# Graph layer on one core: x + h of one row block stored from another buffer, the first load of x in two halves, the last product in two pieces of columns

## The chip, the cores and the metric

The kernel runs on one core of one Trainium2 chip. The metric is the device time of one execution in microseconds (us). Three executions of the kernel before took 1384.38, 1384.48 and 1384.94 us; the median is 1384.48 us. Engines are named as in the profile: PE is TensorE (matmul), PEld its weight load, DVE is VectorE, ACT is ScalarE, POOL is GpSimd, and SP is SyncE, which here only issues DMAs.

## The reference

One layer of a relational graph network with a highway gate, in float32, on N = 1250 nodes with D = 1024 features, E = 20000 edges and R = 8 edge types:

```python
h = relu(layernorm(x))                      # over the 1024 features, no scale or shift
u = h @ root + bias
for r in range(8):                          # mean over the edges of type r into a node
    sums = segment_sum(h[src] * (type == r), dst)
    u += (sums / max(count_r, 1)) @ weight[r]
z = concat([u, h]) @ w_gate + b_gate        # w_gate has 2048 rows
out = x + tanh(u) * z + h * (1 - z)
```

Most of the work is eleven matrix products of 1250 x 1024 by 1024 x 1024: one for each edge type, one with root, and two with the halves of w_gate.

## The kernel before

**Blocks and pairs.** The 1250 rows are ten blocks of 128 (the last has 98). Blocks i and i + 5 are pair i, and are called part 0 and part 1 of the pair. The edge sums are taken after the product: h @ weight[r] is formed for every node and stored in `y`, and a later stage gathers the rows that the edges name and adds them up.

**One product.** `product` multiplies a pair (256 rows) by a 1024 x 1024 matrix with the seven products of a Strassen-like scheme on a 2 x 2 split. The left operand of a pair, `h_op[i]`, is one tile with seven slots of [128, 4 x 128]: the transposed quarters A11, A12, A22 and the sums S1, S2, S3 (which first holds A21) and S4. The function `add` issues the four float32 matmuls of one of the seven; in the profile each matmul has two records, so one add is eight records at L204. The order is A11, S1, S2, S4, S3, A12, A22. Adds gather in banks of PSUM, from which ScalarE and VectorE copy or add the quarters of the result into two row tiles; the last, A22, is taken by the function given as `last`. After each of the seven adds `done` calls `between(j)`, in which the work of other engines is written. There are 55 products, eleven matrices for five pairs, one after another on TensorE. The right operand's sums are made once for each matrix (`make_t1` to `make_t4`, L160 to L172).

**Order.** The order of instructions on each engine is written by hand: it is that of the program text, and the only scheduling is the place at which a piece of work is called. Each engine takes its instructions in order and waits for the semaphores of those it depends on. All loads of x and all stores of rows go over SP's queue.

**The first stage.** The layernorm of all pairs runs beside the first products, from the generator `norms`, which `on` advances by one `yield` after each add. `Normed` holds one block: `xt` its x, `ht` its h. `stats` and `spread` (L388, L392, L393) take mean and deviation, `scale` (L397, L398) the factors, `relu` (L405, on ScalarE) writes h into `ht`, `store` (L410) stores it to `h_dram`, and `with_x` (L414, L415) adds h to x in place and stores the sum to `xh_dram` for the last stage. `both` does this for the two blocks of a pair; `factored` transposes them on TensorE (L180, copied out at L182), and `left` (L189 to L193) makes the sums S1, S2, S4 and S3 on VectorE.

There is little room in SBUF, so blocks use slots of `h_op` tiles that are not yet filled. For pair 2 this matters: x of its first block is loaded into slots S1 and S2 of `h_op[2]` itself, and h of that block is written to `scratch(4, 0)`, slots 0 and 1 of `h_op[4]`. Pair 3's first block later writes its h to the same `scratch(4, 0)`. The second blocks of pairs 2 and 3 share `scratch(4, 1)` in the same way. x of pair 2's second block and of both blocks of pair 3 is in buffers of a pool of three, `xpool`, from which pair 4 takes the buffers for its x and h too.

The order in `norms` around pair 2 is: the x + h of pair 1, then `factored(2)`, the two `with_x` of pair 2, `left(h_op[2])`, the load of x of block 4, and, two yields later, the layernorm of pair 3. The first pair is written by itself ahead of the products, with its relu in two halves; its two blocks are the first loads on SP's queue.

**The last stage.** The eleventh matrix is multiplied with u, which has been gathered by then. `finish` takes half a block's columns of the result, multiplies by one factor and adds another (L1144 and L1145), and `scatter_outs` sends rows to the output with an indirect DMA of POOL (L308). In the last product of all, part 1's first half of the columns comes from the A22 add, straight from PSUM through `last`.

Of the kernel before, what the change touches and what calls it, by code (L numbers as in the profile page):

```python
# [19 lines left out]
def tile_rgcn_highway(  # L20
# [30 lines left out]
    nc = tc.nc  # L51
# [3 lines left out]
    P = 128  # L55
    N, D = x.shape
# [3 lines left out]
    KQ = KC // 2  # L60
    Q = D // 2
    ND = -(-N // P)
    NP = ND // 2
# [16 lines left out]
    A11, A12, A22, S1, S2, S3, S4 = range(7)  # L80
# [4 lines left out]
    def nrows(d):  # L85
        return min(P, N - d * P)
# [18 lines left out]
    xh_dram = dram.tile([N, D], F32, name="xh_dram")  # L105
# [9 lines left out]
    def bank():  # L115
        return psum.tile([P, 512], F32, name="ps", bufs=6)
# [57 lines left out]
    def transposed(aop, part, of, n):  # L174

        for half, to in enumerate(((A11, A12), (A21, A22))[part]):
            p = bank().rearrange("p (k f) -> p k f", k=KQ)
            for i in range(KQ):
                k = KQ * half + i
                nc.tensor.transpose(p[:, i, :n], of[:n, k * P:(k + 1) * P], ident[:n, :n])  # L180
            copy = nc.vector.tensor_copy if half else nc.scalar.copy
            copy(aop[:, to, :, :n], p[:, :, :n])  # L182
            if n < P:
                nc.gpsimd.memset(aop[:, to, :, n:], 0.0)

    def left(aop, part=0):

        if part != 3:
            nc.vector.tensor_add(aop[:, S1], aop[:, A21], aop[:, A22])  # L189
            nc.vector.tensor_sub(aop[:, S2], aop[:, S1], aop[:, A11])  # L190
        if part != 1:
            nc.vector.tensor_sub(aop[:, S4], aop[:, A12], aop[:, S2])
            nc.vector.tensor_sub(aop[:, S3], aop[:, A11], aop[:, A21])  # L193

    def product(aop, w, to, between=lambda j: None, last=nc.scalar.copy):


        c11, c12 = to[0][:, :Q], to[0][:, Q:]
        c21, c22 = to[1][:, :Q], to[1][:, Q:]
        step = [0]  # L200

        def add(b, i, fresh=False):
            for k in range(KQ):
                nc.tensor.matmul(b, aop[:, i, k, :], w.of[i][:, k, :], start=(fresh and k == 0),  # L204
                                 stop=(k == KQ - 1), skip_group_check=True)

        def done():
            between(step[0])
            step[0] += 1

        b, c = bank(), bank()
        add(b, A11, True)
        nc.scalar.copy(c11, b)  # L213
        done()
        add(c, S1, True)
        nc.scalar.copy(c22, c)  # L216
        done()
        add(b, S2)
        nc.scalar.copy(c12, b)  # L219
        done()  # L220
        add(c, S4)
        nc.vector.tensor_add(c12, c12, c)  # L222
        done()
        add(b, S3)
        d = rows.tile([P, Q], F32, name="part", bufs=2)
        nc.scalar.copy(d, b)  # L226
        nc.vector.tensor_add(c22, c22, d)  # L227
        done()
        a = bank()
        add(a, A12, True)  # L230
        nc.vector.tensor_add(c11, c11, a)  # L231
        done()
        add(b, A22)
        last(c21, b)  # L234
        done()

    mats = [weight[r] for r in range(R)] + [root, w_gate[D:, :], w_gate[:D, :]]
# [119 lines left out]
    with ExitStack() as early:  # L357
# [3 lines left out]
        first_part = early.enter_context(ExitStack())  # L361
        xpool = first_part.enter_context(tc.tile_pool(name="xpool", bufs=3))

        def load_x(i, part, t=None):
            d = i + part * NP
            n = nrows(d)
            if t is None:
                t = xpool.tile([P, D], F32, name="xt")
            nc.sync.dma_start(t[:n], x[d * P:d * P + n, :])
            return t  # L370

        def scratch(i, part):

            return h_op[i][:, 2 * part:2 * part + 2].rearrange("p a k f -> p (a k f)")

        class Normed:
# [32 lines left out]
                at = slice(self.d * P, self.d * P + self.n)  # L409
                nc.sync.dma_start(h_dram[at, :], self.ht[:self.n])  # L410

            def with_x(self):
                n = self.n
                nc.vector.tensor_add(self.xt[:n], self.xt[:n], self.ht[:n])  # L414
                nc.sync.dma_start(xh_dram[self.d * P:self.d * P + n, :], self.xt[:n])  # L415

        def both(a, b, parts=1):

            a.stats(0)
            a.stats(1)  # L420
            a.spread()
            b.stats(0)
            a.scale()
            a.relu(parts)
            b.stats(1)
            b.spread()
            b.scale()
            b.relu(parts)

        def factored(i, blocks):  # L430
            for part in range(2):
                transposed(h_op[i], part, blocks[part].ht, blocks[part].n)
# [1 line left out]

        warm = xpool.tile([P, 1], F32, name="warm")
        nc.scalar.activation(warm, eps, AF.Sqrt)
        x0 = [load_x(0, part) for part in range(2)]
        fac[0].load_first()
        fac[0].load_b22()
        x1 = [load_x(1, 0, scratch(NP - 2, 0))]  # L440
# [11 lines left out]
        for name, of, pad in (("dst", dst, G * KEYS), ("typ", etype, R), ("src", src, 0)):  # L452
            t = ix0.tile([P, 2, P], I32, name=f"e_{name}")
# [281 lines left out]
        def norms():  # L735
            yield
            yield
            both(*b1)
            fac[0].make_t4()
            for b in b1:  # L740
                b.store()
            yield
            yield
            factored(1, b1)
            left(h_op[1])
            yield
            for b in b0:
                b.with_x()
            x3 = [load_x(3, part) for part in range(2)]
            b2 = [Normed(2 + part * NP, x2[part], scratch(NP - 1, part)) for part in range(2)]  # L750
            both(*b2)
            yield
            for b in b2:
                b.store()
            yield
            for b in b1:
                b.with_x()
            yield
            factored(2, b2)
            for b in b2:  # L760
                b.with_x()
            left(h_op[2])
            x4 = [load_x(4, 0)]
            yield
            yield
            b3 = [Normed(3 + part * NP, x3[part], scratch(NP - 1, part)) for part in range(2)]
            both(*b3)
            yield
            for b in b3:
                b.store()  # L770
            yield
            factored(3, b3)
            left(h_op[3])
            yield
            for b in b3:
                b.with_x()
            x4.append(load_x(4, 1))
            yield
            for part in range(2):
                b = Normed(4 + part * NP, x4[part], xpool.tile([P, D], F32, name="xt"))  # L780
                b.stats(0)
                b.stats(1)
                b.spread()
                b.scale()
                b.relu()
                b.store()
                yield
                transposed(h_op[4], part, b.ht, b.n)
                b.with_x()
                yield  # L790
            left(h_op[4])
            first_part.close()
# [19 lines left out]
    with ExitStack() as edges_part:  # L812
# [12 lines left out]
        fresh = [GOT]  # L825
# [113 lines left out]
        s, i = next(steps)  # L939
        while s <= R0[1]:  # L940
            step(s, i)
            s, i = next(steps)
# [8 lines left out]
        def with_others(e):  # L951
# [6 lines left out]
            for _ in others:  # L958
# [3 lines left out]
        s, i = beside(with_others(edges(0, range(ND), u_back(0))), sum(K[0]) + 1, s, i,  # L962
                      R0[2] - 1)
# [6 lines left out]
        for g in range(1, G - 1):  # L970
            e = edges(g, range(ND), u_back(g))
            s, i = beside(with_passes(e) if g == G - 2 else e, sum(K[g]) + 1, s, i, R0[g + 2] - 1)
# [4 lines left out]
        with tc.If(passes > 0):  # L977
# [30 lines left out]
            with tc.For_i(0, passes, 1):  # L1008
# [9 lines left out]
                for c in range(NCH):  # L1018
                    n = nedges(c)
# [104 lines left out]
        between = spread(in_turn(late, held()), sum(K[LG]) + 2, 7 * ((NM - 2 - s) * NP + NP - i))  # L1124
        while s < NM - 1:
# [8 lines left out]
            s, i = next(steps, (NM, 0))  # L1134

        for i in range(NP):
            t = [rows.tile([P, D], F32, name="row") for _ in range(2)]

            def finish(part, half, of):
                d = 2 * i + part  # L1140
                n = nrows(d)
                at = slice(half * Q, half * Q + Q)
                to = t[part][:n, at]
                nc.vector.tensor_mul(to, of[:n], place_of("d", i, part)[:n, at])  # L1144
                nc.vector.tensor_add(to, to, place_of("z", i, part)[:n, at])  # L1145

            def beside_u(j):
                if i == 0 and j == 0:
                    fac[NM - 1].make_t4()
                gate_rows(i, j)  # L1150
                if j == 1:
                    scatter_outs()
                if i + 2 < NP:
                    gate_load(i + 2, j)
                if j == (3 if i else 5):
                    finish(0, 1, t[0][:, Q:])
                if j == (4 if i else 5):
                    finish(1, 1, t[1][:, Q:])
                if j == 5:
                    finish(0, 0, t[0][:, :Q])  # L1160
                    outs.append((2 * i, t[0]))
                    if i == NP - 1:
                        scatter_outs()
                if i + 1 < NP:
                    gate_u(i + 1, j)

            product(h_op[i % 2], fac[NM - 1], t, between=beside_u,
                    last=lambda to, b: finish(1, 0, b))
            outs.append((2 * i + 1, t[1]))
        scatter_outs()  # L1170
# [22 lines left out]
```

## Time and profile before

| | us |
|---|---|
| median of three executions | 1384.48 |
| the profiled execution | 1385.41 |
| its span in the profile | 1383.6 |
| PE busy | 1364.6 (99%) |
| DVE busy | 861.1 (62%) |
| POOL busy | 630.1 (46%) |
| ACT busy | 339.4 (25%) |
| mean granted TensorE clock | 0.996 of full |

The profile is of one execution of the program, and its times count from the start of the span. Busy times are sums over the instructions of an engine. A line of the waits names the engine and the instruction that waited, what released it, the time in total, how often, and the longest. A line of the timeline has the start, the busy time, the engine, the line of the kernel, the operation, what it writes and reads, and in brackets the idle time before it and what ended that. The granted clock is the share of full speed that TensorE's clock was given. The matmuls L204 are 3080 records with 1343.5 us.

### The profile page before, as it was taken

How to read it: one execution, taken by the hardware profiler on the slowest of the kernel's cores; microseconds unless marked ns; L12 is line 12 of the kernel's file. 1: busy time of each engine (PE TensorE's matmuls, PEld its weight loads, DVE VectorE, ACT ScalarE, POOL GpSimd, SP SyncE). 2: the span in 40 equal slices, each digit the busy share in tenths (PEclk: the TensorE clock that was granted, in tenths of full speed). 3: DMA queues.
4: the chain of work that ended last, by engine and by line, in shares of the span. 5: the costliest groups of instructions: out<-in, count | busy, mean ns of one | idle time of the engine just before them, and what ended most of it. 6: DMA issues, size and time to landing. Idle time of an engine off the chain costs nothing. (4 is left out here: it accounts for less than half of the span.)

```text
span 1383.6 us, 11973 instructions
## 1 busy us (share of the span) xinstructions
PE 1364.6 (99%) x3562; PEld 615.9 (45%) x3562; DVE 861.1 (62%) x1658; ACT 339.4 (25%) x721; POOL 630.1 (46%) x567
## 2 busy tenths in 40 slices
PE   7899999999999999999999999999999999999998
PEld 4444444444444444444444444444444444444443
DVE  7855877887767826456355575654346564557975
ACT  3335656566521111111111111111111111121220
POOL 0002755665560644556575454544417433425641
PEclk9999999999999999999999999999999999999999
DMA  9654764775545256269878756787659845656861
GB/s 328 257 180 114 165 132 129 162 163 138 98 111 179 62 155 201 63 221 220 241 244 288 261 176 217 281 300 273 218 175 334 293 153 180 206 177 237 293 201 57
DMA packets 109863, 272.73 MB, mean 197 GB/s; under 512 B 25890, under 2 KB 27920, under 8 KB 109664
## 3 DMA queue, kind: packets, MB, share of 16 engines
q0 software_dynamic: 48864, 128.60, 28.8%
q1 hardware_dynamic: 39808, 101.38, 24.7%
q10 hardware_dynamic: 21120, 41.95, 9.8%
q8 instruction: 28, 0.46, 0.1%
q14 instruction: 43, 0.35, 0.1%
HBM read 214.20 MB, written 80.65 MB: 213 GB/s over the span
## 5 line engine op out<-in xcount | busy, mean ns | idle before, releaser
L204 PE MATMUL ps<-w,h_op 128*128 128x512 f32 x3080 | 1343.5, 595 | 0.5 <-DVE w L172 0.4
L204 PEld LDWEIGHTS ps<-w,h_op 128*128 128x128 f32 x3080 | 578.7, 190 | 695.4 <-issue 690.8
L845 DVE SCALAR_TENSOR_TENSOR u<-got,w_of,u 128x1024 f32<-128x1024 f32 (+1 forms) x192 | 246.0, 1283 | 200.3 <-DMA got<-y,idx 197.9
L837 POOL DMA_INDIRECT got<-y,idx x202 | 249.3, 1234 | 230.7 <-DVE u L845 140.7
L664 POOL DMA_INDIRECT table<-row_col,at_i x157 | 177.1, 1128 | 159.8 <-DVE at_i L660 68.7
L222 DVE TENSOR_TENSOR row<-row,ps 128x512 f32<-128x512 f32 x55 | 37.7, 685 | 106.3 <-PE ps L204 71.5
L226 ACT COPY part<-ps 128x512 f32<-128x512 f32 x55 | 32.2, 585 | 269.5 <-PE ps L204 269.5
L234 ACT COPY row<-ps 128x512 f32<-128x512 f32 x50 | 29.3, 585 | 255.3 <-PE ps L204 249.6
L213 ACT COPY row<-ps 128x512 f32<-128x512 f32 x55 | 32.1, 584 | 166.7 <-PE ps L204 158.7
L227 DVE TENSOR_TENSOR row<-row,part 128x512 f32<-128x512 f32 x55 | 37.9, 689 | 46.8 <-ACT part L226 46.7
L219 ACT COPY row<-ps 128x512 f32<-128x512 f32 x55 | 32.1, 584 | 137.7 <-PE ps L204 137.7
L216 ACT COPY row<-ps 128x512 f32<-128x512 f32 x55 | 32.1, 584 | 133.3 <-PE ps L204 129.2
L308 POOL DMA_INDIRECT u_dram<-u,node x20 | 29.2, 1462 | 65.5 <-DVE u L845 63.3
L650 DVE SCALAR_TENSOR_TENSOR junk<-k_bc,key_col,before 128x128 f32<-128x128 int32 x157 | 54.9, 350 | 4.2
L339 POOL DMA_INDIRECT node_dram<-ids,pos_i x30 | 37.7, 1256 | 43.5 <-issue 43.5
L718 DVE SCALAR_TENSOR_TENSOR junk<-v_bc,val,one 128x1280 bf16<-128x1280 f32 x30 | 46.5, 1550 | 8.8 <-DMA v_bc<-val_dram 8.1
L590 DVE TENSOR_TENSOR seen<-seen,ps_n 128x110 f32<-128x110 f32 x157 | 42.1, 268 | 15.5 <-PE ps_n L585 11.5
L567 ACT ACTIVATE is_lo<-io,less_lo 128x128 bf16<-128x128 f32 x157 | 50.1, 390 | 0.7 <-DVE row L227 0.7
L231 DVE TENSOR_TENSOR row<-row,ps 128x512 f32<-128x512 f32 x55 | 37.5, 682 | 19.1 <-PE ps L204 19.1
L302 POOL DMA_INDIRECT u<-u_dram,node x20 | 21.7, 1087 | 48.4 <-DMA u_dram<-u,node 34.0
L160 DVE TENSOR_TENSOR w<-w,w 128x2048 f32<-128x2048 f32 x11 | 25.2, 2291 | 29.9 <-PE ps L204 29.3
L302 POOL DMA_INDIRECT idx<-table,node_key x30 | 34.4, 1145 | 9.1 <-issue 7.9
(159 smaller groups left out, 720.8 us busy)
## 6 DMA issues: line engine op xcount, KB each, us to landing
y<-row SPq DMA_DIRECT2D x72, 512.0 KB, 5.0
w<-in_L_gnn_weight_dram ACTq DMA_DIRECT2D x28, 1024.0 KB, 8.4
k_bc<-keys_dram SPq DMA_DIRECT2D x39, 256.0 KB, 4.9
l_bc<-los_dram SPq DMA_DIRECT2D x39, 256.0 KB
w<-in_L_gnn_w_gate_dram ACTq DMA_DIRECT2D x8, 1024.0 KB
hr_dram<-row SPq DMA_DIRECT2D x9, 512.0 KB, 7.3
z_dram<-row SPq DMA_DIRECT2D x9, 512.0 KB, 6.0
w<-in_L_gnn_weight_dram SPq DMA_DIRECT2D x4, 1024.0 KB
```

The source lines that it names most:

```text
L204: nc.tensor.matmul(b, aop[:, i, k, :], w.of[i][:, k, :], start=(fresh and k == 0), stop=(k == KQ - 1), skip_group_check=True)
L222: nc.vector.tensor_add(c12, c12, c)
L227: nc.vector.tensor_add(c22, c22, d)
L302: nc.gpsimd.indirect_dma_start(out=to, out_offset=None, in_=of, in_offset=bass.IndirectOffsetOnAxis(ap=at, axis=0))
L339: ins = nc.gpsimd.indirect_dma_start(out=node_dram[g][:, :], out_offset=bass.IndirectOffsetOnAxis(ap=pos_i[:, g, d:d + 1], axis=0), in_=id ...
L567: nc.scalar.activation(is_lo[:, i, :], io, AF.Abs, bias=less_lo[:, c0 + i:c0 + i + 1])
L590: nc.vector.tensor_add(seen[j][:, i, :], was, p[:, i, :])
L650: nc.vector.scalar_tensor_tensor(junk, o["k_bc"][:, i, :], key_col[:, c:c + 1], before, op0=OP.is_equal, op1=OP.mult, accum_out=rank[:, c: ...
L664: ins = nc.gpsimd.indirect_dma_start(out=table[:, :], out_offset=bass.IndirectOffsetOnAxis(ap=at_i[:n, i:i + 1], axis=0), in_=row_col[:n, ...
L718: nc.vector.scalar_tensor_tensor(junk, v_bc[:, g, :], val[:, c:c + 1], one.to_broadcast([P, KEYS]), op0=OP.is_gt, op1=OP.mult, accum_out=p ...
L837: nc.gpsimd.indirect_dma_start(out=t[:n], out_offset=None, in_=y[g][:, :], in_offset=bass.IndirectOffsetOnAxis(ap=at[:n, d, k:k + 1], axis=0),
L845: nc.vector.scalar_tensor_tensor(u[:n], t[:n], w, u[:n], op0=OP.mult, op1=OP.add)
```

## The change

Three edits. First, `with_x` can be given the tile to which it writes x + h. Pair 2's first block writes it over its own h, in `scratch(4, 0)`, and no longer over its x, in slots S1 and S2 of `h_op[2]`; its store to `xh_dram` reads from there. (All other blocks keep the old place.) Second, the first block's x is loaded in two DMAs of 512 columns instead of one of 1024. Third, the last product's A22 add is issued as two pieces of 256 columns, each four matmuls and each followed by its own `finish`; `finish` now takes the first column and the width instead of the half.

```diff
-            def with_x(self):
+            def with_x(self, to=None):
                 n = self.n
-                nc.vector.tensor_add(self.xt[:n], self.xt[:n], self.ht[:n])
-                nc.sync.dma_start(xh_dram[self.d * P:self.d * P + n, :], self.xt[:n])
+                to = self.xt if to is None else to
+                nc.vector.tensor_add(to[:n], self.xt[:n], self.ht[:n])
+                nc.sync.dma_start(xh_dram[self.d * P:self.d * P + n, :], to[:n])
...
             factored(2, b2)
-            for b in b2:
-                b.with_x()
+            b2[0].with_x(b2[0].ht)
+            b2[1].with_x()
             left(h_op[2])
...
-        def load_x(i, part, t=None):
+        def load_x(i, part, t=None, pieces=1):
...
-            nc.sync.dma_start(t[:n], x[d * P:d * P + n, :])
+            for j in range(pieces):
+                at = slice(j * D // pieces, (j + 1) * D // pieces)
+                nc.sync.dma_start(t[:n, at], x[d * P:d * P + n, at])
...
-        x0 = [load_x(0, part) for part in range(2)]
+        x0 = [load_x(0, part, pieces=2 - part) for part in range(2)]
...
-        def add(b, i, fresh=False):
+        def add(b, i, fresh=False, at=slice(0, Q)):
             for k in range(KQ):
-                nc.tensor.matmul(b, aop[:, i, k, :], w.of[i][:, k, :], start=(fresh and k == 0),
-                                 stop=(k == KQ - 1), skip_group_check=True)
+                nc.tensor.matmul(b[:, at], aop[:, i, k, :], w.of[i][:, k, at],
+                                 start=(fresh and k == 0), stop=(k == KQ - 1),
+                                 skip_group_check=True)
...
-        add(b, A22)
-        last(c21, b)
+        for j in range(pieces):
+            at = slice(j * Q // pieces, (j + 1) * Q // pieces)
+            add(b, A22, at=at)
+            if last:
+                last(c21[:, at], b[:, at], at.start)
+            else:
+                nc.scalar.copy(c21, b)
...
-            def finish(part, half, of):
+            def finish(part, c0, of):
...
-                at = slice(half * Q, half * Q + Q)
+                at = slice(c0, c0 + of.shape[-1])
...
             product(h_op[i % 2], fac[NM - 1], t, between=beside_u,
-                    last=lambda to, b: finish(1, 0, b))
+                    last=lambda to, b, c0: finish(1, c0, b), pieces=1 + i // (NP - 1))
```

More of the change, by code (lines that the diff above doesn't have):

```diff
@@ L193, in left, with product @@
             nc.vector.tensor_sub(aop[:, S3], aop[:, A11], aop[:, A21])
-    def product(aop, w, to, between=lambda j: None, last=nc.scalar.copy):
+    def product(aop, w, to, between=lambda j: None, last=None, pieces=1):
         c11, c12 = to[0][:, :Q], to[0][:, Q:]
@@ L1155, in beside_u @@
                 if j == (3 if i else 5):
-                    finish(0, 1, t[0][:, Q:])
+                    finish(0, Q, t[0][:, Q:])
                 if j == (4 if i else 5):
-                    finish(1, 1, t[1][:, Q:])
+                    finish(1, Q, t[1][:, Q:])
                 if j == 5:
```

## The prediction

> **What bounds the kernel now.** I read the page's busy table first, then what TensorE (PE) waited for, then the timeline of each wait.
>
> ```profile
> PE 1364.6 (99%) x3562; PEld 615.9 (45%) x3562; DVE 861.1 (62%) x1658; ACT 339.4 (25%) x721; POOL 630.1 (46%) x567
> PE ps L180 <- ACT h_op L405: 11.5, 3, 7.6
> PE ps L204 <- DVE w L172: 0.4, 1, 0.4
> ```
>
> TensorE is busy for 1364.6 of 1383.6 us, so only idle or slow TensorE time can be won. Its waits, over the whole span, are three at the transposes L180, for the normalised rows of L405 (7.6 us is the start; 3.10 and 0.81 are in pair 3), and 0.4 us for one factor. The last columns of the page's slices and the tail's timeline add some 7 us after TensorE's last matmul (1376.7).
>
> Pair 3's wait is where the changed line acts. VectorE (DVE), in the timeline:
>
> ```profile
> 51.27 1.22 DVE L414 TENSOR_TENSOR xt<-xt,h_op 128x1024 f32<-128x1024 f32 x1
> 56.56 0.69 DVE L189 TENSOR_TENSOR h_op<-h_op 128x512 f32<-128x512 f32 x1 [4.07 <-DMA xh_dram<-h_op]
> 60.50 1.28 DVE L388 BATCH_NORM_STATS2 st<-xt 128x6 f32<-128x512 f32 x2
> ```
>
> L189 writes pair 2's left sums over S1, from which x + h is still being stored: VectorE stands for 4.07 us until that store lands (56.44 in the landing records). Everything after it on VectorE is late, pair 3's statistics at 60.50 too. TensorE, and the windows (us, then busy time and count of PE, PEld, DVE, ACT, POOL; granted clock, DMA share, GB/s):
>
> ```profile
> 64.22 1.09 PE L180 MATMUL ps<-ident,h_op 128*128 128x128 f32 x8 [3.10 <-ACT h_op L405]
> 66.12 1.97 PE L180 MATMUL ps<-ident,h_op 128*128 128x128 f32 x8 [0.81 <-ACT h_op L405]
> 67.88 12.61 PE L204 MATMUL ps<-w,h_op 128*128 128x512 f32 x24
> 80.33 1.04 PE L180 MATMUL ps<-ident,xt 128*128 128x128 f32 x8
> 61.00:64.20 3.20, 0.11 (x1) 0.00 (x0) 2.58 (x8) 1.57 (x3) 0.00 (x0) 1.00 0.00 0
> 65.30:72.20 6.90, 6.09 (x15) 3.51 (x15) 6.50 (x15) 2.31 (x4) 0.00 (x0) 0.51 0.33 134
> ```
>
> TensorE idles 3.10 and 0.81 us, and from 65.36 to 72.18 its clock is half: 8 transposes take 1.97 instead of 1.09 us, and 24 matmul records 12.61 where three adds of 3.43 us, the usual spacing, are 10.3. The stall costs a second time there.
>
> [...]
>
> **Part 1, the target of x + h.** The addition keeps its size (1.21 us) and its store. Removed: 4.07 us of L189's wait. Its new start is bounded by VectorE itself: 51.27 + 1.22 = 52.49, so the sums and the queue behind them (L190, L192, L193, three copies L533, L222, the statistics) come up to 4.07 earlier; I take 4.04. L222 also needs TensorE's S4 add: TensorE is done with A12, two adds later, at 60.95 (its clean slot), so S4 ended at 60.95 − 2 × 3.43 = 54.1, before L222's new place, 55.87. Added: the target buffer is shared. The addition of b2[0] now waits for the store of h, landed 48.01 against 50.14: nothing, by 2.1 us. The relu of b3[0] writes the same buffer and now waits for the x + h store, 56.44. Behind it on ScalarE (ACT) stand the relu of b3[1] and the copy L226, which empties the bank that the A22 add fills.
>
> ```profile
> 62.92 1.24 ACT L405 ACTIVATE h_op<-xt,less,rs 128x1024 f32<-128x1024 f32 x1 [0.51 <-DVE less L398]
> 64.83 1.24 ACT L405 ACTIVATE h_op<-xt,less,rs 128x1024 f32<-128x1024 f32 x1 [0.48 <-ACT sd L393]
> ```
>
> With 4.04 off, the first relu is ready at 58.88, 2.4 us after the landing, so the wait costs nothing; it ends 60.12, before TensorE is free at 60.95. The second ends 66.07 − 4.04 = 62.03. Transposes: part 0 at 60.95 to 61.97, part 1 at 62.05 to 62.9; the A22 add starts at 62.89 (L226, 0.57 after the second relu, is done at 62.6) instead of 67.88: 5.0 us. With only about 2 us between adds the clock should stay full: two sets of transposes in pairs 1 and 2 (1.91 us for 16, at 28.65 and 44.13) ran at full clock. So three adds are 10.3 instead of 12.45 (67.88 to 80.33): 2.15 more, and pair 4's transposes could start at 73.19, 7.1 us earlier.
>
> What is late next: pair 4's first relu, 78.30 before, writes the row buffer of b3[1], whose x + h store landed 76.99. With the shift that is 72.95, so relu at 73.0 to 74.24 and transposes at about 74.3: 1.1 us of idle[...]. The gain is 80.33 − 74.3 = **6.0 us**. Bounds: if that store follows TensorE more closely (it is issued after the A22 add's turn), it keeps 7.1; if the load of x of pair 4's second part (79.34, shifted 75.3, needed 77.1) or the store lags 2 us more, 4.0.
>
> **Part 2, x in two loads.** One more issue on SP's queue (0.43 us each there), which moves every later load by that, and halves the first.
>
> ```profile
> 4.23 1.29 DVE L388 BATCH_NORM_STATS2 st<-xt 128x6 f32<-128x512 f32 x2 [4.23 <-DMA xt<-in_x_dram]
> 5.67 0.64 DVE L388 BATCH_NORM_STATS2 st<-xt 128x6 f32<-128x512 f32 x1
> 6.61 1.52 ACT L405 ACTIVATE h_op<-xt,less,rs 128x512 f32<-128x512 f32 x2 [0.52 <-DVE less L398]
> ```
>
> The first half may land at 3.5, so one statistic (0.65) starts early and the second can end up to 0.6 earlier. But b0[1]'s first statistic stands ahead of b0[0]'s scale in VectorE's order, and its load (5.43) comes no earlier, 0.4 later if the extra issue binds. So relu moves from 6.61 by −0.25 to +0.2; I take **−0.15**. The first matmul also needs b11 (8.34) and t3 (10.95), whose factors are made from 11.87 on: 0.9 us of cover for the extra issue's 0.4. If the statistic weren't in the way, 0.6.
>
> **Part 3, the last A22 add in two pieces.**
>
> ```profile
> 1376.74 0.69 DVE L1144 TENSOR_TENSOR row<-ps,h_op 98x512 f32<-98x512 f32 x1 [1.30 <-PE ps L204]
> 1377.47 0.69 DVE L1145 TENSOR_TENSOR row<-row,h_op 98x512 f32<-98x512 f32 x1
> 1378.47 0.95 POOL L308 DMA_INDIRECT out_dram<-row,node  x1 [1.67 <-DVE row L1145]
> ```
>
> The add starts at 1373.11, its slot ends at 1376.54, and VectorE follows 0.2 later. Eight matmuls of 256 columns (0.21 each, half of 3.43/8) are a piece of 1.72 us. Both pieces are in one bank, and in the changed program's order the second piece's first matmul waits for the first piece's multiplication. So piece 1 ends at 1374.83; VectorE is then in L1145 (1374.76 to 1375.45); its multiplication takes 0.42[...] and ends 1375.79. Piece 2 runs from 1375.9 to 1377.6, its two operations end 0.2 + 0.42 + 0.05 + 0.42 later, at 1378.69 against 1378.16: **+0.5 us**. Bounds: −0.5 without that wait, +0.8 with 0.1 more at each of three handings over.
>
> **Sum.** −6.0 − 0.15 + 0.5 = −5.65. Against the profiled execution's span of 1383.6: 1377.95. That execution took 1385.41; the runs' median is 1384.48, 0.9 lower, and I take the change off that: **1378.8 us**.
>
> **Rivals.** (a) *More:* pair 4's wait or the tail's doesn't occur, −7.3: 1377.2. For it: both rest on margins of about 1 us. (b) *The wait moves and takes part:* the addition or the relu of b3[0] waits for its store, or pair 4 waits 2 us longer: part 1 gives 3.4 instead of 6.0, −3.05: 1381.4. That is also how the change would not do what it says. The store begins to count when it lands after 59.55 (the second relu has 0.67 us of room behind the first), 3.1 later than it did, and costs that much at about 63. The margin speaks against it. (c) *Given back later:* every gain must pass the one other wait, L172 at 1025.56, on which the product at 1028 waits 0.38 us. VectorE there stood behind gathers:
>
> ```profile
> DVE u L845 <- DMA got<-y,idx: 61.8, 16, 14.0
> DVE w L172 <- DVEq L977: 6.5, 1, 6.5
> ```
>
> If the gathers were bound by something that doesn't move, the wait grows to about 6 us, and only the tail's 0.5 is left: 1385.0. Against: they are issued in the order of the program from stores paced by TensorE, so they shift with it. (d) *Slower:* the same place,[...] the clock halves once more for 6.8 us, which loses half of that, 3.4, on top of the tail's 0.5: 1388.4.[...]
>
> **Chances.** Forecast 0.72 (own range 1377.3 to 1380.6); (a) 0.08; (b) 0.08; (c) 0.07; (d) 0.05. A difference under 0.2%, 2.8 us, can't be told from none: the border is 1381.7. (b) straddles it: 0.06 below, 0.02 above. Faster 0.86, same 0.09, slower 0.05. The range 1376.9 to 1381.5 holds the forecast, (a) and most of (b), some 0.85.
>
> **What would show it.** L189 of pair 2 following the addition by its own length, without a DMA as releaser; the first relu of b3 near 58.9 with VectorE's L398 as releaser, not a DMA; no window between 60 and 75 at half clock; L180 of pair 4 near 74.3, with an idle of about 1 us; L204 at the end with a wait of 1 us on the first piece's multiplication; the wait at 1028, some 6 us earlier, still under a microsecond. I am wrong if the relu of b3[0] names the x + h store, if half clock remains, or if L172's wait grows.

## The result, and the profile after

| | before | after |
|---|---|---|
| median of 22 executions each, us | 1384.47 | 1382.09 |
| lowest to highest | 1383.27 to 1387.67 | 1380.38 to 1384.27 |
| the profiled execution, us | 1385.41 | 1380.38 |
| its span | 1383.6 | 1378.6 |
| PE busy | 1364.6 | 1361.7 |

The ratio is 0.9981, with a 95% interval of 0.9974 to 0.9988: 2.6 us faster, between 1.7 and 3.6. (Differences in us that are given below with a ratio are that ratio times 1384.5.) The forecast was 1378.8 with a range that ended at 1381.5, 0.6 us below the time measured; its sum was a gain of 5.65 us. The two profiled executions differ by 5.0 us, which is twice what the medians differ by. That gap is the question of this study.

In the profile after, each step of the first edit is where the forecast put it. What TensorE waited for, over the whole span (time in total, times, longest; a wait of 0.2 us for ScalarE elsewhere is left out):

```profile
PE ps L180 <- ACT h_op L413: 8.0, 1, 8.0
PE ps L180 <- ACT xt L413: 1.2, 1, 1.2
PE ps L204 <- DVE row L1153: 0.8, 1, 0.8
```

Pair 3's waits are gone. In their place stand 1.2 us ahead of pair 4's transposes and 0.8 us in the tail. The timeline of VectorE and ScalarE around pair 3:

```profile
51.76 1.22 DVE L423 TENSOR_TENSOR xt<-xt,h_op 128x1024 f32<-128x1024 f32 x1
52.90 0.69 DVE L189 TENSOR_TENSOR h_op<-h_op 128x512 f32<-128x512 f32 x1
56.84 1.28 DVE L396 BATCH_NORM_STATS2 st<-xt 128x6 f32<-128x512 f32 x2
...
59.21 1.24 ACT L413 ACTIVATE h_op<-xt,less,rs 128x1024 f32<-128x1024 f32 x1 [0.46 <-DVE less L406]
73.67 1.24 ACT L413 ACTIVATE xt<-xt,less,rs 128x1024 f32<-128x1024 f32 x1 [1.44 <-DMA xh_dram<-xt]
```

L189 follows the addition at once, and the relu of pair 3 is released by VectorE, not by the store that it could now have waited for. Pair 4's relu waits 1.44 us for the store from the buffer it takes over. TensorE, and the window in which it had half its clock before:

```profile
61.44 2.06 PE L180 MATMUL ps<-ident,h_op 128*128 128x128 f32 x16
63.33 10.47 PE L204 MATMUL ps<-w,h_op 128*128 128x512 f32 x24
74.96 1.09 PE L180 MATMUL ps<-ident,xt 128*128 128x128 f32 x8 [1.16 <-ACT xt L413]
...
65.30:72.20 6.90, 6.90 (x17) 3.04 (x16) 6.39 (x10) 1.44 (x3) 0.20 (x1) 1.00 0.30 121
```

The clock is full (1.00), and pair 4's transposes come at 74.96 instead of 80.33. But this profile begins late, too. The start, and the tail (POOL's line is the last store):

```profile
3.37 0.69 DVE L396 BATCH_NORM_STATS2 st<-xt 128x6 f32<-128x512 f32 x1 [3.37 <-DMA xt<-in_x_dram]
4.56 0.69 DVE L396 BATCH_NORM_STATS2 st<-xt 128x6 f32<-128x512 f32 x1 [0.49 <-DMA xt<-in_x_dram]
6.07 0.69 DVE L396 BATCH_NORM_STATS2 st<-xt 128x6 f32<-128x512 f32 x1 [0.57 <-DMA xt<-in_x_dram]
7.06 1.52 ACT L413 ACTIVATE h_op<-xt,less,rs 128x512 f32<-128x512 f32 x2 [1.23 <-DVE less L406]
...
1369.73 0.42 DVE L1153 TENSOR_TENSOR row<-ps,h_op 98x256 f32<-98x256 f32 x1
1370.20 1.99 PE L204 MATMUL ps<-w,h_op 128*128 128x256 f32 x8 [0.84 <-DVE row L1153]
1372.24 0.42 DVE L1153 TENSOR_TENSOR row<-ps,h_op 98x256 f32<-98x256 f32 x1 [1.63 <-PE ps L204]
1372.69 0.42 DVE L1154 TENSOR_TENSOR row<-row,h_op 98x256 f32<-98x256 f32 x1
1373.43 0.95 POOL L314 DMA_INDIRECT out_dram<-row,node  x1 [2.26 <-DVE row L1154]
```

The first half of x is there at 3.37, but the second block's x (the statistic at 6.07, 5.67 before) is later, and the first relu moves from 6.61 to 7.06.

To compare stages between executions, I take from each trace the start of ScalarE's first copy in each of the 55 products, which follows the first add of the product. The table gives it, less the same copy in the profile before, for the second product (behind the start), the fourth (behind pairs 3 and 4), the 32nd and the last; then the span less 1383.6. "Pairs 3, 4" is the fourth less the second. All runs of the study are in it. Each line is one execution.

| kernel | first transposes at | 2nd | 4th | pairs 3, 4 | 32nd | 55th | span |
|---|---|---|---|---|---|---|---|
| before | 7.56 | 0 | 0 | 0 | 0 | 0 | 0 |
| after | 8.02 | 0.48 | -5.31 | -5.79 | -5.01 | -5.63 | -5.0 |
| before, again | 7.73 | 0.10 | 0.18 | 0.08 | 1.02 | 2.94 | 3.0 |
| x + h alone | 7.74 | 0.59 | -5.25 | -5.84 | -3.85 | -4.47 | -4.4 |
| split load alone | 8.26 | 1.04 | -0.20 | -1.24 | 6.14 | 5.52 | 5.5 |
| tail alone | 7.48 | 0.65 | -1.40 | -2.05 | -1.05 | -1.67 | -1.0 |
| spare matmuls | 7.50 | 0.69 | -0.95 | -1.64 | -0.98 | -1.60 | -1.6 |
| x + h, pair 4's buffer | 7.51 | 0.28 | -6.16 | -6.44 | -5.95 | -6.57 | -6.5 |
| tail, finishes last | 7.56 | 0.39 | -0.75 | -1.14 | -0.41 | -1.03 | -0.7 |
| one small load more | 7.49 | 0.51 | -0.48 | -0.99 | 0.16 | -0.46 | -0.5 |
| x + h and split | 9.27 | 2.08 | -3.72 | -5.80 | -3.12 | -3.74 | -3.7 |
| x + h and tail | 7.53 | 0.30 | -5.54 | -5.84 | -5.44 | -6.06 | -5.4 |
| x + h, split, seven loads | 8.96 | 1.66 | -4.12 | -5.78 | -3.75 | -3.15 | -3.2 |
| spare matmuls, pair 4's buffer | 7.56 | -0.02 | -2.69 | -2.67 | -2.71 | -3.33 | -3.3 |

### The profile page after: what moved, and what is told of

Same layout as the page of the kernel before. It is cut to its first block, busy times and chain, and to the rows that moved or that the text cites. A ratio compares the mean times of both kernels' runs of the same rounds, so it can differ in the third digit from the quotient of the medians.

```text
span 1378.6 us, 11994 instructions
## 1 busy us (share of the span) xinstructions
PE 1361.7 (99%) x3570; PEld 615.9 (45%) x3570; DVE 861.0 (62%) x1660; ACT 338.9 (25%) x721; POOL 628.8 (46%) x567
## 4 chain that ended last, share of the span: by engine, by line
PE 84%; issue 4%; DVE 3%; DMA 2%; POOL 1%; ACT 1%; POOLq 0%; DVEq 0%; ACTq 0%
PE ps L204 83%; DMA w<-in_L_gnn_weight_dram 1%; PE ps_n L594 1%; DMA got<-h_dram,node 0%; DMA u<-last_dram 0%; DVE row L1153 0%; DVE h_op L1091 0%; PE ps L180 0%; DVE u L1054 0%; POOL out_dram L314 0%; POOL got L308 0%; DVE row L1154 0%; PE ps_q L645 0%; DMA xh_dram<-xt 0%; DVE w L1091 0%
## 5 line engine op out<-in xcount | busy, mean ns | idle before, releaser
L204 PE MATMUL ps<-w,h_op 128*128 128x512 f32 (+1 forms) x3088 | 1341.4, 593 | 1.0 <-DVE row L1153 0.8
L846 POOL DMA_INDIRECT got<-y,idx x202 | 253.0, 1252 | 230.3 <-DVE u L854 150.5
L223 DVE TENSOR_TENSOR row<-row,ps 128x512 f32<-128x512 f32 x55 | 37.7, 685 | 95.9 <-PE ps L204 61.7
```

Of the source, the lines that this page charges most:

```text
L204: nc.tensor.matmul(b[:, at], aop[:, i, k, :], w.of[i][:, k, at], start=(fresh and k == 0), stop=(k == KQ - 1), skip_group_check=True)
L846: nc.gpsimd.indirect_dma_start(out=t[:n], out_offset=None, in_=y[g][:, :], in_offset=bass.IndirectOffsetOnAxis(ap=at[:n, d, k:k + 1], axis=0),
```

## The experiments

**The kernel before, again.** No edit; its single executions are what is looked at.

> The kernel before, unchanged, run again under its own label to see single executions. Theory A (each execution of the kernel before loses 3.4 us to the half clock behind pair 3's wait): every span has a mean clock near 0.996, ratio 1.000. Theory B ([...]the half clock comes in only a part of the executions): some spans have a clock of 0.999 and are about 3.4 us shorter than those with 0.996; with the median 1384.5 and the changed kernel's profile at 1380.4, that would explain why the medians differ by 2.4 and the two profiles by 5.0.

Ratio 1.0002 (0.9993 to 1.0010). Theory B is nearer. Over the 127 executions of the kernel before that ran beside the experiments or in this run, the mean granted clock and the span go together:

| mean clock | executions | median span |
|---|---|---|
| 0.999 | 12 | 1381.4 |
| 0.998 | 53 | 1382.5 |
| 0.997 | 38 | 1383.2 |
| 0.996 and 0.995 | 24 | 1384.0 |

The profiled execution before (0.996) belongs to the fifth with the lowest clock: a large loss by the clock was taken for the usual one. The changed kernel has 0.998 to 1.000 in all 22. So the two profiles show the difference between a poor execution of before and, with 1380.38 as the lowest of 22, the best one of after.

**Each edit alone.** Three kernels, each the changed one with two edits undone. x + h alone:

```diff
-        x0 = [load_x(0, part, pieces=2 - part) for part in range(2)]
+        x0 = [load_x(0, part) for part in range(2)]
...
-                    last=lambda to, b, c0: finish(1, c0, b), pieces=1 + i // (NP - 1))
+                    last=lambda to, b, c0: finish(1, c0, b), pieces=1)
```

> Only the target of x + h of pair 2's first block is changed; first x in one load, last add in one piece. By the forecast's sum this alone is worth -6.0 us against before in a profile; by the changed kernel's profile (start +0.5, tail +0.5) -6.0 too, so about 1.0 us faster than the changed kernel. If the gain of the median is limited by executions that wait elsewhere (theory C, the loss sits after 100 us), it is -3 to -3.5 in the median with the clock at 0.999.

The split load alone:

```diff
-            b2[0].with_x(b2[0].ht)
+            b2[0].with_x()
...
-                    last=lambda to, b, c0: finish(1, c0, b), pieces=1 + i // (NP - 1))
+                    last=lambda to, b, c0: finish(1, c0, b), pieces=1)
```

> Only the first x in two loads. Forecast: -0.15 us (-0.25 to +0.2). By the changed kernel's profile, in which the first transposes start at 8.02 instead of 7.6 because the second block's load lands later: +0.4 to +0.5. The second relu of pair 0 and all behind it should move by that in the trace.

The tail alone:

```diff
-        x0 = [load_x(0, part, pieces=2 - part) for part in range(2)]
+        x0 = [load_x(0, part) for part in range(2)]
...
-            b2[0].with_x(b2[0].ht)
+            b2[0].with_x()
```

> Only the last A22 add in two pieces. Forecast: +0.5 us (-0.5 to +0.8), with TensorE waiting about 0.8 us on the first piece's multiplication, as in the changed kernel's profile.

x + h alone: 0.9968 (0.9956 to 0.9980), 4.4 us faster. Split alone: 1.0013 (1.0006 to 1.0020), 1.8 us slower. Tail alone: 1.0009 (1.0001 to 1.0017), 1.2 us slower. So the first edit gains and the two others lose part of it. For x + h, -4.4 lies between the two expectations, -6.0 and -3 to -3.5. There are only six executions, and the interval (2.8 to 6.1 us faster) excludes neither. The further runs with x + h, and the traces, narrow it down.

The kernel with the tail alone has the wait of pair 3, and in its profile the stage took 2.05 us less than in the profile before. TensorE there, and the windows:

```profile
64.43 3.59 PE L180 MATMUL ps<-ident,h_op 128*128 128x128 f32 x16 [2.66 <-ACT h_op L413]
67.86 10.46 PE L204 MATMUL ps<-w,h_op 128*128 128x512 f32 x24
78.86 1.09 PE L180 MATMUL ps<-ident,xt 128*128 128x128 f32 x8 [0.54 <-ACT xt L413]
...
64.30:68.00 3.70, 3.57 (x17) 3.24 (x18) 3.08 (x13) 2.98 (x6) 0.00 (x0) 0.55 0.59 245
68.00:72.00 4.00, 4.00 (x11) 1.76 (x10) 3.83 (x7) 0.57 (x2) 0.00 (x0) 1.00 0.09 36
```

Here the half clock is one window (64.19 to 67.60 by the trace's clock records) and falls on the transposes. The 24 matmul records run in 10.46 us, as in the kernel after, where the profile before had 12.61; and pair 4 already waits 0.54 us for its store. In the six profiles whose pair 3 is as before, the stage took 0.08 more to 2.05 less than in the first, 0.89 less on average. In the five that write x + h over h and leave pair 4 alone, it is always 5.78 to 5.84 less. The edit's gain in this stage is therefore 4.9 us on average, from 3.7 to 5.9, and the profile before showed the top of it.

What goes with one half window here and two there can be read from the same traces. Their clock records lie on a grid of 3.41 us (in the profile before they last 54.61, 6.83 and 1307.31 us, 16, 2 and 383 times 3.413; in the profile after 1365.33 us, 400 times), whose place differs from profile to profile. TensorE's busy time in the grid's windows at pair 3:

| kernel | window that half clock follows | busy in it | busy in the first half window | half windows |
|---|---|---|---|---|
| before | 61.94 to 65.36 | 1.09 | 2.65 | 2 |
| before, again | 62.00 to 65.41 | 0.89 | 2.67 | 2 |
| one small load more | 60.48 to 63.89 | 1.14 | 2.60 | 2 |
| tail, finishes last | 60.18 to 63.60 | 1.33 | 2.55 | 2 |
| split load alone | 63.94 to 67.36 | 1.24 | 3.41 | 1 |
| tail alone | 60.78 to 64.19 | 0.99 | 3.17 | 1 |

In the first four, some of pair 3's waiting still lies in the first half window, and a second follows. In the last two, TensorE works through most of it.

**Without the half clock.** The wait stays, but TensorE has something to do in it:

```diff
+            spare = bank()
+            for k in range(3):
+                nc.tensor.matmul(spare, h_op[1][:, A11, k, :], fac[0].of[A11][:, k, :],
+                                 start=(k == 0), stop=(k == 2), skip_group_check=True)
             factored(3, b3)
```

> The kernel before with three spare float32 matmuls (six records, 2.6 us, their result read by nobody) put ahead of pair 3's transposes, so that TensorE works while it waits for the relu; the wait of VectorE stays. Theory A (the half clock behind the wait is one or two free windows of 3.41 us, one as a rule): no window at half clock between 60 and 75, transposes of pair 3 still at about 64.2, the relu's wait 0.5 us, and the median 1 to 2 us lower than before. If two windows were the rule, as in the profile before: 2.5 to 3 us lower. If the clock weren't the cause of the slow matmuls: no change.

The trace is as theory A wanted it (L774 are the spare matmuls):

```profile
61.65 2.74 PE L774 MATMUL ps<-w,h_op 128*128 128x512 f32 x6
64.89 1.09 PE L180 MATMUL ps<-ident,h_op 128*128 128x128 f32 x8 [0.51 <-ACT h_op L405]
66.80 1.09 PE L180 MATMUL ps<-ident,h_op 128*128 128x128 f32 x8 [0.81 <-ACT h_op L405]
67.73 10.46 PE L204 MATMUL ps<-w,h_op 128*128 128x512 f32 x24
79.32 1.09 PE L180 MATMUL ps<-ident,xt 128*128 128x128 f32 x8 [1.13 <-ACT xt L405]
```

The transposes and matmuls run at full clock (1.00 from 61 to 80 us). But the ratio is 0.9998 (0.9989 to 1.0006): 0.2 us, at most 1.5, where theory A expected 1 to 2. What the clock gives back at 78 us is in part waited away at 79.32, where pair 4's relu waits for its buffer.

With x + h alone the clock is full too (1.00 from 60 to 80 us), and pair 4 waits as long (1.13 us); what differs is pair 3's wait. It is worth 4.2 us (4.4 less 0.2; in the stage of the two profiles 5.84 less 1.64, also 4.2). The forecast had 3.9 for it, the two waits of 3.10 and 0.81. For the clock and pair 4's new wait together it had 1.95: 2.15 for the matmuls and 0.9 for the transposes at half clock (in its 5.0), less 1.1. Here the two are worth 0.2, at most 1.5. So the wait was sized rightly, and the clock was not.

The mean clock says the same of many executions: 0.9974 over the 127 of the kernel before, 0.9988 over the 13 with spare matmuls. The difference is about 2 us of lost clock per execution (an estimate from clocks that are given to 0.001), where the two half windows of the profile before lost 3.4.

**Pair 4's buffer.** The h of pair 4's first block goes elsewhere, on top of x + h alone:

```diff
-                b = Normed(4 + part * NP, x4[part], xpool.tile([P, D], F32, name="xt"))
+                b = Normed(4 + part * NP, x4[part], xpool.tile([P, D], F32, name="xt")
+                           if part else scratch(4, 1))
```

> Only the target of x + h changed (as in the run with that edit alone), and h of pair 4's first block written to slots 2 and 3 of the fifth operand tile instead of a buffer whose store has just been issued. If the wait of 1.1 us before pair 4's transposes is that buffer's: the relu 1.0 us earlier, transposes with next to no idle, and about 1.0 us less than with that edit alone: some 5.4 us faster than before.

0.9961 (0.9948 to 0.9975), 5.4 us faster, median 1379.12: the quickest kernel of the study, and faster than the changed one.

```profile
72.81 1.24 ACT L413 ACTIVATE h_op<-xt,less,rs 128x1024 f32<-128x1024 f32 x1 [0.79 <-DVE less L406]
74.11 1.09 PE L180 MATMUL ps<-ident,h_op 128*128 128x128 f32 x8 [0.51 <-ACT h_op L413]
```

The relu is released by VectorE and no DMA. Half a microsecond of TensorE's wait stays, since the relu is 1.24 us long and the statistics end just before. The stage is 0.60 us shorter than with x + h alone, less than the 1.0 expected.

The same buffer under the spare matmuls:

> The kernel before with the three spare matmuls in pair 3's wait, and h of pair 4's first block in slots 2 and 3 of the fifth operand tile. With the spare matmuls alone the median fell by only 0.2 us, and pair 4's transposes waited 1.13 us for a store. If that wait swallowed what the full clock had given (theory A with the later wait): 1.0 to 1.4 us faster than before, transposes of pair 4 with next to no idle. If the half clock cost nothing as a rule: 0.2 us again.

0.9995 (0.9986 to 1.0003), 0.7 us. The wait is 0.50 instead of 1.13, and the profiled stage took 1.03 us less than with the spare matmuls alone. That fits a swallowed gain in the trace; in the median it doesn't reach the 1.0 to 1.4, and the profiled execution (1380.3) is the shortest of thirteen with a median span of 1382.7. Where the other twelve lose isn't known: only one execution is traced.

**The tail without its wait.** On the tail alone, both pieces are multiplied before either is finished:

```diff
         for j in range(pieces):
             at = slice(j * Q // pieces, (j + 1) * Q // pieces)
             add(b, A22, at=at)
+        for j in range(pieces):
+            at = slice(j * Q // pieces, (j + 1) * Q // pieces)
             if last:
                 last(c21[:, at], b[:, at], at.start)
```

> Only the last add in two pieces, but both pieces of matmuls ahead of the two finishes, so no matmul waits for VectorE. From the last add's start to the end of the span: before 10.5 us, with the wait 11.1 to 11.2. If the wait is the cost: 10.8 (four short operations of VectorE instead of two long ones are 0.3 more). If short matmuls themselves cost: 11 or more.

This kernel has a single execution, so only its trace is used, not its time.

```profile
1375.73 0.42 DVE L1155 TENSOR_TENSOR row<-ps,h_op 98x256 f32<-98x256 f32 x1 [1.31 <-PE ps L204]
1376.53 0.42 DVE L1155 TENSOR_TENSOR row<-ps,h_op 98x256 f32<-98x256 f32 x1
1376.98 0.43 DVE L1156 TENSOR_TENSOR row<-row,h_op 98x256 f32<-98x256 f32 x1
```

From the last product's copy to the end of the span, this execution takes 0.28 us more than before, and the three with the wait (after, tail alone, x + h and tail) 0.61 to 0.64 more, by the traces that the columns "55th" and "span" round. So nearly half of the tail's cost is the four short operations, and the rest the wait of 0.8 us, which the overlap of the first piece's finish doesn't pay for. Cutting the add gains nothing in either form.

**The split and the order of semaphores.** The split costs 1.8 us by itself, and the 22 executions of the changed kernel spread over 3.9 us, the 17 of x + h with the split over 4.0; the six of x + h alone over 1.1, the seven of x + h with the tail over 1.7. One idea was that every later DMA now takes the next of the eight semaphores in turn, so that waits fall on other transfers. The kernel before with one small load more tests it:

```diff
             nc.sync.dma_start(t, far)
+        extra = ix0.tile([1, 1], I32, name="extra")
+        nc.sync.dma_start(extra, dst[None, :1])
```

> The kernel before with one more load of 4 bytes on SP's queue, after the first loads and stores, so that every later DMA takes the next of the eight semaphores in turn, as with the first x in two loads, while the start is as before. Theory S1 (the split costs its 0.45 us at the start and the rest of its measured 1.8 us is spread between executions): 0.0 us. Theory S2 (what costs is that later waits for a semaphore fall on other transfers): 1.0 to 1.5 us slower.

Beside it, the split and the tail each on top of x + h. First x + h with the split, against the changed kernel:

```diff
-                    last=lambda to, b, c0: finish(1, c0, b), pieces=1 + i // (NP - 1))
+                    last=lambda to, b, c0: finish(1, c0, b), pieces=1)
```

> x + h over h and first x in two loads, last add in one piece. With x + h alone measured at -4.4 us: if the split costs only the later landing of the second block's x (theory S1), 0.4 to 0.5 us less gain, -4.0. If it costs what the run with the split alone measured, 1.8: -2.5.

Then x + h with the tail:

```diff
-        x0 = [load_x(0, part, pieces=2 - part) for part in range(2)]
+        x0 = [load_x(0, part) for part in range(2)]
```

> x + h over h and the last add in two pieces, first x in one load. From the traces the tail is 0.65 us longer: -3.7. By the run with the tail alone in the median, 1.2 to 1.4: -3.0 to -3.2.

And x + h with the split and seven small loads, which bring the old semaphores back:

```diff
             nc.sync.dma_start(t, far)
+        for k in range(7):
+            extra = ix0.tile([1, 1], I32, name=f"extra{k}")
+            nc.sync.dma_start(extra, dst[None, :1])
```

> As the run before last (x + h over h, first x in two loads), with seven loads of 4 bytes more after the first loads and stores, so that from there on every DMA uses the same of the eight semaphores as in the kernel before. Theory S1: as without them, -4.0. Theory S2 (the moved semaphores cost about 1.3): back to -4.0 where the run without them is at -2.5.

| kernel | ratio | 95% interval | us |
|---|---|---|---|
| one small load more | 1.0003 | 0.9994 to 1.0011 | +0.4 |
| x + h and split | 0.9979 | 0.9971 to 0.9986 | -2.9 |
| x + h and tail | 0.9971 | 0.9960 to 0.9982 | -4.0 |
| x + h, split, seven loads | 0.9978 | 0.9971 to 0.9985 | -3.0 |

The semaphores fall as the cause (S2): with their old order the time is the same. On top of x + h the split costs 1.5 us and the tail 0.4, and S1's 0.45 is too small, too. The traces show where most of it goes. VectorE's start with x + h and split:

```profile
3.42 0.69 DVE L396 BATCH_NORM_STATS2 st<-xt 128x6 f32<-128x512 f32 x1 [3.42 <-DMA xt<-in_x_dram]
5.00 0.69 DVE L396 BATCH_NORM_STATS2 st<-xt 128x6 f32<-128x512 f32 x1 [0.88 <-DMA xt<-in_x_dram]
7.33 0.69 DVE L396 BATCH_NORM_STATS2 st<-xt 128x6 f32<-128x512 f32 x1 [1.39 <-DMA xt<-in_x_dram]
```

The second block's statistic, which stands ahead of the first block's scale, starts at 7.33 here, at 5.67 in the kernel before. By the landing records that block's x is complete at 5.37 to 5.63 in ten profiles without the split, and at 6.05, 6.29, 7.30 and 7.00 in four with it; its 16 parts landed within 0.3 to 0.5 us without, within 0.75 to 1.8 us with it. The first block gains little: its first half is complete at 3.35 to 3.42, but its second at 4.24 to 5.76, where the whole block was at 4.00 to 4.38. The first transposes follow: 7.48 to 7.74 in ten profiles without, 8.02, 8.26, 9.27 and 8.96 with it. That is 1.1 us on average. It differs from one execution to the next, by up to 1.25 us among these four, which fits the wider spread. The 0.4 to 0.7 us between this and the medians isn't accounted for, and lies within their intervals. Why the transfers are slower isn't shown by these runs.

## Why the prediction was wrong

**What held.** The wait of L189 went, and nothing took its place at pair 3. The relu of b3[0] waits for VectorE, not for the shared buffer; pair 4 waits for its store (1.16 us, 1.1 forecast); the transposes of pair 4 came 5.79 us earlier than in the profile before, taken from the second product's start, with 6.0 forecast. VectorE's short operation took 0.42 us in the profile after, as the forecast had it (an addition of 256 columns, L522, has 424 ns in the profile before), and the tail's wait is 0.84 with 1 forecast, its cost 0.6 with 0.5. (The forecast let the first multiplication end at 1375.79; 0.42 us after 1375.45 is 1375.87, with which its own sum gives 0.6.)

**Step 1, the half clock: wrong.** "So three adds are 10.3 instead of 12.45: 2.15 more" is true of the profile before, but not of executions in general: with the tail alone the same records took 10.46. The forecast took the place of the clock's windows in one profile for that in all executions. The clock of 127 executions spreads from 0.995 to 0.999, with 2.6 us between the median spans of the ends. Spare matmuls in the wait, which remove the half clock, gain 0.2 us (1.5 at most) where the forecast's terms for the clock and pair 4's wait give 1.95; with 0.2 in their place, 6.0 becomes about 4.3. The average of the traces' stage gives 4.9. x + h alone measured 4.4.

**From the profile to the median: wrong for the same reason.** The profile of before was 0.9 us above its median and the forecast took the change off as if this part were common to both kernels. The clock table suggests that it came in part from the clock, whose loss at pair 3 the change takes away; this is not shown for that one execution.

**Step 2, the split: wrong in sign and size.** -0.15 was forecast, with +0.2 as the upper bound; it costs about 1.1 us in the traces and 1.5 to 1.8 in the medians. The text had the extra issue's 0.4 us and the statistic that stands in the way, and still let only half of that through. The rest, up to 1.3 us, is a slower landing that no view of before shows; the upper bound left no room for it.

**Step 3, the tail: right.** Its cost followed from the order of the program and two durations.

**The sum with measured terms** is -4.4 for x + h, +1.5 for the split and +0.4 to 0.6 for the tail: -2.5 to -2.3, where -2.6 (-3.6 to -1.7) was measured.

**The rivals.** (b), half of the gain, has about the size but neither its place nor its cause. (c) and (d) did not come at 1028: no wait is left there. Whether a longer wait at that place would have halved the clock, as (d) had it, is not shown. Between the 41st and the 42nd product, where it was, the profile after is 0.6 us shorter than that of before. The only other profile with the wait is the second one of the kernel before; six with the old x + h don't have it either, so this part isn't shown to be the edit's. A loss of their kind does exist elsewhere: VectorE runs behind TensorE in the edge stage, and in some executions TensorE waits for a factor that VectorE makes, some 250 us before the place that the forecast named. In the profile of the split alone:

```profile
PE ps L204 <- DVE w L164: 2.5, 1, 2.5
777.74 22.76 PE L204 MATMUL ps<-w,h_op 128*128 128x512 f32 x49 [2.54 <-DVE w L164]
```

Between the 31st and the 32nd product this execution lost 4.26 us, x + h alone 0.70, x + h with the split 0.46, the tail alone 0.10, the others nothing. VectorE's addition L223 (L222 before) in the 31st product started 26.4, 25.3 and 25.5 us behind its undisturbed place, three adds of 3.43 us after the product's first copy, in the three that lost most (the time that TensorE lost is in it), 24.2 in the tail alone, and 22.5 or less in all others. The lag differs between executions of kernels with the same code there (16.6 and 22.5 us in the two profiles of the kernel before), so it can add spread to every kernel here, and it is not shown that the change moves it.

## What to carry to other kernels

The stall of TensorE here had a fixed part, the wait (3.91 us in the profile before), and a part that depended on the place of the clock's windows (two of 3.41 us at half clock in four profiles, one in two): before the second is counted as a gain, look at the granted clock of several executions, not at one profile. Splitting a load that the first instructions need was not free here: what mattered was when the last part of the next load landed (at 6.05 to 7.30 us instead of 5.37 to 5.63). When a wait on a store is removed, look for the next buffer that is taken over from a store; giving pair 4 another buffer saved 0.6 us in the profiles, where the other two edits of the change cost time.

## What was not expected of the hardware

- Half clock followed windows that had work in them. In the profile before, the 3.41 us ahead of 65.36 hold 2.27 us of idle time and 1.1 us of transposes. In the profile of the split alone a wait of 2.54 us was followed by half clock from 777.33 to 780.74, with about 2.1 us idle in the 3.41 us ahead of it. The waits at pair 4 of 1.16 us (after) and 1.13 us (x + h alone) were followed by none: the clock from 70 to 80 us is 1.00 in both.
- At full clock, the six windows of the table above, with 0.89 to 1.33 us busy, and the one ahead of 777.33, with about 1.3, were each followed by half clock; in the profile after, two with 2.25 us (from 72.71) and 1.99 us busy (from 1369.78) were followed by full clock. At half clock, the four windows of the table with 2.55 to 2.67 us busy were followed by another at half clock, and the two with 3.17 and 3.41 us by full clock. The busy times are the trace's, in which the ends of matmuls are modelled.
- In the profile before, the clock's records begin at 10.74 us, with full clock; until then TensorE had run only transposes, from 7.56 on.
- With the first transfer in two halves, the transfer behind it landed more unevenly: the second block's last part landed 0.75 to 1.8 us after its first in four profiles, against 0.3 to 0.5 us in ten.
